# Sampling products on all 16 array tiles, column coordinates by broadcast DMA, one PSUM bank for convolution and tokens

## The chip, the cores and the metric

The kernel runs on one core of a Trainium2 chip. Times are device microseconds (us) of one execution. The core has five engines that run beside one another and meet at semaphores: TensorE (PE, with its weight loads shown as PEld), VectorE (DVE), ScalarE (ACT), GpSimd (POOL) and SyncE (SP), which here issues the DMAs. PE writes to PSUM, eight banks of 512 float32 values in each of 128 partitions; PE's array can be split into tiles of 32 rows by 32 columns. Every engine works through its own instructions in the order in which they are written.

## The reference

The input is 16 images of 64 x 64 pixels with 128 channels. Layer 0 normalises each image by groups (`_gn`), computes by a 3 x 3 convolution two offsets for every pixel and channel, and samples the normalised image bilinearly at the shifted coordinates; the result is added to the input. Layer 1 works on the 4096 tokens of an image: an attention over the 16 values of a head, with a layer norm before it, and then a mixture of experts.

```python
offsets = lax.conv_general_dilated(x, W, ...) + b            # 3x3, 128 -> 256 channels
off = offsets.transpose(0, 3, 1, 2).reshape(-1, h, w, 2)
coords = off.reshape(bc, -1, 2) + grid[None]                 # bc = image x channel
c0 = jnp.clip(coords[..., 0], 0.0, w - 1); c1 = jnp.clip(coords[..., 1], 0.0, h - 1)
# bilinear: four neighbours of (c0, c1) in the channel's own 64 x 64 plane
mapped = vals_t + (vals_b - vals_t) * f1
...
x = x + _L0_conv_ref(_gn(x), ...)
t = t + _L1_attn_ref(_ln_t(t), ...)
t = t + _L1_ffn_ref(_ln_t(t), ...)    # top 8 tokens per expert, two matmuls, scatter back
```

## The kernel before

The class `Images` takes the 16 images one after another: the first and the last written out, the fourteen between in a loop. An image has eight chunks `k` of 512 points (8 columns of the image by 64 rows); a chunk has 32 steps, called slots, and a step samples four channels (two `a`, two `h`). So an image has 256 slots, and the run 4096.

**Sampling (`sample`).** Bilinear sampling is written as sums with hat functions: the value is the sum over rows r and columns c of hat(c0 - r) hat(c1 - c) D(r, c). A hat is a ramp cut off at 0 and 1; the image is stored as differences (`xr`) so that one ramp per row and one per column is enough. A step does this:
- *Row block* (L543, tile `rps`): four bf16 matmuls spread the row coordinates of the channels, held in three bf16 parts (`parts`), over 32 rows per half image and subtract the row number.
- *Row ramp*: ACT reads the bank (L565) and ramps again in SBUF (L569); in every fourth step (`s % 4 == 2`) DVE does it in one instruction (L561). The result is `rhat`.
- *Column block* (L555, `jps`), in every second step for two steps: four bf16 matmuls do the same for the column coordinates, and ACT ramps them into `chat` (L563, L568).
- *Product block* (L501, `yps`): float32 matmuls of 32 x 32 tiles multiply the row hats with a window of 32 columns of `xr`. `half(j, 0)` does the upper half of the image's rows (row groups 0 and 1 of the array), `half(j, 1)` the lower half (row groups 2 and 3), accumulated on the upper one in the same bank. The upper half of step j+1 and the lower half of step j are issued together, on eight tiles and in two banks. An explicit dependency keeps a lower half behind the DVE product of the step before, so that only one row group writes a bank at a time.
- *Product with the column hats* (L526): DVE multiplies `yps` with min(`chat`, 1) into `prod`.
- *Sums* (L534, `acc`): every fourth step, four matmuls sum the products of four steps over the columns.

The row block of slot i is issued three slots ahead of the product of its step.

**The other work.** `conv` computes the next chunk's offsets: 18 float32 taps (L414) in two groups of nine, then DVE instructions that make and clip the coordinates, split them into bf16 parts, and DMAs that bring them to `parts`. `tokens` does layer norm, qkv, attention and gate logits of a finished chunk: transposes and matmuls on PE, large elementwise instructions on POOL (L687, L688, L692), exp on ACT (L700), sums on DVE (L701, L706). `prep` loads and normalises the next image; `tail` chooses the top 8 tokens of the image before and pools them. All these are functions put into a `Plan` under a slot number. In slot i, `plan.emit(i)` comes first, then the step's own instructions, then `plan.emit(i + 0.5)`, mostly token and convolution matmuls. So the order on each engine is this hand-made order.

**PSUM before.** Pool `bcp` has two buffers of two banks each, shared in turn by row blocks, column blocks and all token, prep and tail matmuls (`bank`); `ps_y` has two banks for the products, `ps_c` one for the convolution, `ps_a` one for the sums.

After the images, `experts` runs the two expert matmuls and `combine` scatters the results back and writes the output.

Of the kernel before, what the change touches and what calls it, by code (L numbers as in the profile page):

```python
# [18 lines left out]
P = 128  # L19
B, IMG, C = 16, 64, 128  # L20
NPIX = IMG * IMG
NCH = 8
# [15 lines left out]
TAIL_AT = [84, 88, 92, 112, 116, 120, 124, 144]  # L38
PREP_AT = [150, 154, 158, 162, 176, 180, 184, 188]
# [85 lines left out]
class Images:  # L125
# [8 lines left out]
    def __init__(self, ctx, tc, x, conv_w, conv_b, w_qkv, b_qkv, w_proj, b_proj, gate_w, gate_b,  # L134
# [7 lines left out]
        self.pc_d = dram.tile([C, 3, 2, CHW], BF16, name="pc_d")  # L142
# [5 lines left out]
        self.bcp = ctx.enter_context(tc.tile_pool(name="bcp", bufs=2, space=PSUM))  # L148
        self.ps_y = ctx.enter_context(tc.tile_pool(name="ps_y", bufs=2, space=PSUM))
        self.ps_c = ctx.enter_context(tc.tile_pool(name="ps_c", bufs=1, space=PSUM))  # L150
# [33 lines left out]
        gps = self.bank("gps")[:, 0, :E]  # L184
# [47 lines left out]

# [7 lines left out]
        self.selw = [keep([P, 8, 2 * WIN], f"selw{i}", BF16) for i in range(2)]  # L240

        self.parts = [keep([P, 4, 2, CHW], f"parts{i}", BF16) for i in range(2)]
# [6 lines left out]
        for o in range(2):  # L249
            nc.vector.memset(self.red[o], 0.0)  # L250
            rflat = self.red[o].rearrange("p t m -> p (t m)")
            for u in range(4):
                nc.vector.memset(
                    rflat[32 * u : 32 * (u + 1), 16 * (u // 2 ^ o) + u % 2 :: 34], 1.0)
# [11 lines left out]
        self.pc = keep([P, 3, 2, CHW], "pc", BF16)  # L266
# [3 lines left out]
        self.xl = keep([P, NA, C], "xl")  # L270
# [22 lines left out]
    def bank(self, name):  # L293

        return self.bcp.tile([P, 2, 512], F32, name=name, tag="bc")


    def prep(self, b, turns, slot, norm_slot):
# [4 lines left out]
        def load(t):  # L303
            nc.sync.dma_start(self.xl, xt[t])

        def turn(t):
            st["ps"] = self.bank("xps")
            for a in range(NA):
                nc.tensor.transpose(st["ps"][:, 0, P * a : P * (a + 1)], self.xl[:, a, :], self.ident)

        def stats(t):
            v = self.big[:, CHW * t : CHW * (t + 1)]
            nc.scalar.copy(v, st["ps"][:, 0, :])
# [14 lines left out]
        def group2():  # L328
            st["ps"] = self.bank("gps")[:, 0, :]
# [7 lines left out]
        def group4():  # L337
            st["ps"] = self.bank("gps")[:, 0, :]
# [33 lines left out]
        def down(r):  # L372
            st = self.xl.rearrange("p a c -> p (a c)").rearrange("p (i j) -> p i j", j=IMG)
# [32 lines left out]
    def conv(self, k, slot):  # L406
# [3 lines left out]
        def tap(s, t):  # L410
            if t == 0:
                st["ps"] = self.ps_c.tile([P, CHW], F32, name="cps", tag="c")
# [25 lines left out]
        def clip():  # L438
            nc.vector.tensor_scalar(self.cd, self.cd, 0.0, float(IMG - 1), ALU.max, ALU.min)
            nc.gpsimd.tensor_tensor(  # L440
                self.selw[k % 2].rearrange("p t (h j) -> p (t h) j", h=2),
                bcast(self.pat, 2, WIN),
                bcast(self.sgn[:, window(k) : window(k) + WIN], 1, 16), ALU.mult,
            )
# [597 lines left out]
```

## Time and profile before

| | us |
|---|---|
| median of 3 runs | 14970.91 |
| lowest and highest | 14949.8 and 14973.13 |
| profiled execution | 14941.81 |
| its span, first to last instruction | 14940.0 |
| mean granted TensorE clock | 0.836 |

Read from the trace, the images begin at about 107 us and the expert stage at about 14,198 us; the combine stage runs from 14,593 us to the end. Counting from the first DVE product of one image to that of the next, an image takes 871 to 883 us (the first 812, from 120.3 to 932.2), so a chunk takes 109 us on average and a slot 3.4. The page gives PE 78% of the span busy, DVE 61%, ACT 59%, POOL 55%. In its list of groups the number after the bar is the busy time of all instructions of a group in us, then the mean of one in ns, then the idle time of that engine just before them and what ended it. Matmuls of different tiles overlap, so the busy time of a group is not its count times its mean.

### The profile page before, as it was taken

Reading aid. Unit: us, or ns where it says so; the run is one execution under the profiler, and the core shown is the slowest. Engines: PE = TensorE matmul, PEld = TensorE weight load, DVE = VectorE, ACT = ScalarE, POOL = GpSimd, SP = SyncE. Lnnn points to the kernel's source line nnn. Section 1 sums busy time; section 2 is a strip of 40 time slices with the busy share of each in tenths; the row PEclk is TensorE's granted clock in tenths of the full one; section 3 lists DMA queues with packets and bytes.
Section 4 is the critical chain, followed back from the end, with each engine's and each line's share of the span. In section 5 each row is a group of like instructions: output and inputs, shape, how many; then the busy total and the mean of one; then the engine's idle time right before and its main releaser. Section 6 shows DMA issues by size and latency. Waiting matters only on the chain. (4 is left out here: it accounts for less than half of the span.)

```text
span 14940.0 us, 334280 instructions
## 1 busy us (share of the span) xinstructions
PE 11673.5 (78%) x144834; PEld 5414.2 (36%) x144834; DVE 9074.3 (61%) x13110; ACT 8855.4 (59%) x10818; POOL 8272.1 (55%) x5147
## 2 busy tenths in 40 slices
PE   6878777787877778777777878777777777778597
PEld 2333333333333333333333333333333333333276
DVE  4666666666666665666666566666656666665502
ACT  4666666666666666666666666666666666666400
POOL 2666565655556555565565555656566565656500
PEclk8888888888888888888888888888888888888655
DMA  1111111111111111111111111111111111111027
GB/s 43 26 38 32 35 34 34 35 30 38 32 35 34 33 35 30 33 37 35 34 33 33 34 32 36 37 30 36 30 38 32 35 37 27 37 29 35 21 92 227
DMA packets 467476, 595.25 MB, mean 40 GB/s; under 512 B 174080, under 2 KB 275200, under 8 KB 463936
## 3 DMA queue, kind: packets, MB, share of 16 engines
q1 hardware_dynamic: 429504, 539.43, 14.1%
q10 hardware_dynamic: 36480, 34.12, 0.9%
q8 instruction: 1157, 18.96, 0.5%
q14 instruction: 335, 2.74, 0.1%
HBM read 321.19 MB, written 252.18 MB: 38 GB/s over the span
## 5 line engine op out<-in xcount | busy, mean ns | idle before, releaser
L501 PE MATMUL yps<-rhat,xr 32*32 32x352 f32 (+2 forms) x98304 | 4115.0, 423 | 1299.1 <-DVE prod L526 863.1
L565 ACT ACTIVATE rhat<-rps,one 128x704 f32<-128x704 f32 x3072 | 2593.7, 844 | 3680.5 <-PE rps L543 3675.7
L526 DVE SCALAR_TENSOR_TENSOR prod<-chat,yps 128x512 f32<-128x512 f32 x4096 | 2791.8, 682 | 3035.9 <-PE yps L501 2708.7
L501 PEld LDWEIGHTS yps<-rhat,xr 32*32 32x32 f32 x98304 | 2245.6, 115 | 3471.2 <-issue 1039.1
L692 POOL TENSOR_TENSOR ev<-sc,qkv 128x1024 f32<-128x1024 f32 x1024 | 2426.1, 2369 | 1117.8 <-ACT sc L700 1012.2
L569 ACT ACTIVATE rhat<-rhat,one 128x704 f32<-128x704 f32 x3072 | 2707.1, 881 | 66.4
L414 PE MATMUL cps<-pad,wconv 128*128 128x512 f32 x4608 | 2402.0, 639 | 22.9 <-DVE far L433 16.7
L687 POOL TENSOR_TENSOR sc<-qkv 128x1024 f32<-128x1024 f32 x1024 | 1991.7, 1945 | 241.2 <-POOLq L865 106.8
L688 POOL TENSOR_TENSOR sc<-sc,top 128x1024 f32<-128x1024 f32 x1024 | 1999.5, 1953 | 82.8 <-DVE top L681 2.6
L543 PE MATMUL rps<-parts,sel 64*64 64x352 bf16 x16384 | 1538.7, 365 | 186.1 <-ACT rhat L565 136.1
L675 POOL TENSOR_TENSOR top<-qkv,kmm 128x512 f32<-128x512 f32 x128 | 136.5, 1066 | 2652.5 <-ACT qkv L671 2646.6
L706 DVE TENSOR_REDUCE att<-ev 128x64 f32<-128x1024 f32 x1024 | 1234.1, 1205 | 352.1 <-POOL ev L692 352.1
L534 PE MATMUL acc<-prod,red 128*32 128x512 f32 x8192 | 1434.0, 774 | 0.0
L563 ACT ACTIVATE chat<-jps 128x1024 f32<-128x1024 f32 x1024 | 1041.9, 1018 | 647.7 <-PE jps L555 644.0
L701 DVE TENSOR_REDUCE den<-sc 128x64 f32<-128x1024 f32 x1024 | 1241.6, 1212 | 278.4 <-ACT sc L700 275.9
L543 PEld LDWEIGHTS <-sel 64*64 64x64 bf16 x16384 | 497.2, 107 | 2278.7 <-issue 2230.7
L700 ACT ACTIVATE sc<-sc 128x1024 f32<-128x1024 f32 x1024 | 1071.6, 1047 | 211.9 <-POOL sc L688 211.9
L414 PEld LDWEIGHTS cps<-pad,wconv 128*128 128x128 f32 x4608 | 788.3, 193 | 861.0 <-issue 843.4
L568 ACT ACTIVATE chat<-jps 128x1024 f32<-128x1024 f32 x1024 | 1038.0, 1014 | 0.0
L586 POOL TENSOR_SCALAR rstd<-mv 128x4 f32<-128x4 f32 x256 | 93.7, 366 | 1661.2 <-DVE mv L583 1661.2
L555 PE MATMUL jps<-parts,selw 64*64 64x512 bf16 x8192 | 886.3, 420 | 117.9 <-ACT tr L716 88.5
L561 DVE TENSOR_SCALAR rhat<-rps 128x704 f32<-128x704 f32 x1024 | 903.7, 883 | 47.7 <-PE rps L543 47.7
(142 smaller groups left out, 10598.3 us busy)
## 6 DMA issues: line engine op xcount, KB each, us to landing
pc_d<-pc SPq DMA_DIRECT2D x128, 768.0 KB
parts<-pc_d SPq DMA_DIRECT2D x768, 128.0 KB
xl<-in_x_dram SPq DMA_DIRECT2D x128, 256.0 KB
xn_d<-xl SPq DMA_DIRECT2D x128, 256.0 KB
xr<-xn_d SPq DMA_DIRECT2D x512, 64.0 KB
xres<-in_x_dram SPq DMA_DIRECT2D x256, 128.0 KB
t_d<-t SPq DMA_DIRECT2D x256, 128.0 KB
xin_d<-xln SPq DMA_DIRECT2D x128, 256.0 KB
```

The lines of the kernel that those rows point to most:

```text
L414: nc.tensor.matmul(st["ps"], self.wconv[:, t, s, :], self.pad[:, kh + par : kh + par + 63 : 2, kw + 16 * col : kw + 16 * col + 16], start= ...
L501: mm = nc.tensor.matmul(ys[j][v : v + 32, lo:hi], self.xr[t][g : g + 32, 2 * m + a, w0 : w0 + WIN], rows[j][g : g + 32, a, lo - SEG0 * s : ...
L526: prod = nc.vector.scalar_tensor_tensor(prods[j], cols[j - j % 2][:, j % 2, :], 1.0, ys.pop(j), ALU.min, ALU.mult)
L534: nc.tensor.matmul(self.acc[32 * m : 32 * (m + 1), :], self.red[m % 2][:, t, :], prods.pop(j - 4 + m), start=(t == 0), stop=(t == 7),)
L543: nc.tensor.matmul(ps[64 * sg : 64 * (sg + 1), a, :NSEG], self.sel[64 * a : 64 * (a + 1), t, sg].rearrange("p h i -> p (h i)"), parts[64 * ...
L565: ramp = nc.scalar.activation(rows[i], ps[:, :, :NSEG], AF.Relu, bias=self.one, scale=-1.0)
L569: nc.scalar.activation(rows[i], rows[i], AF.Relu, bias=self.one, scale=-1.0)
L687: nc.gpsimd.tensor_tensor(sc, bcast(qa[:, hs], 3, HD), bcast(ka[:, hs], 2, HD), ALU.mult)
L688: nc.gpsimd.tensor_tensor(sc, sc, bcast(top[:, hs], 3, HD), ALU.subtract)
L692: nc.gpsimd.tensor_tensor(self.ev, self.sc[i % 2], bcast(va[:, hs], 2, HD), ALU.mult)
L701: add(begin[i] + 3, lambda i=i: nc.vector.tensor_reduce(den[:, 4 * i : 4 * (i + 1)], self.sc[i % 2], AX.X, ALU.add))
L706: add(begin[i] + 2, lambda j=j: nc.vector.tensor_reduce(att[:, 4 * j : 4 * (j + 1)], self.ev, AX.X, ALU.add))
```

## The change

It rewrites the sampling loop in pairs of slots and moves the PSUM banks:
- Product blocks: the upper halves of two steps and the lower halves of the two steps before them are issued together, in four banks (`ps_y` with 4 buffers), and the column tile is now `32 * (2 * a + (h ^ m % 2))`, so that two neighbouring steps use different tiles of a row group. Together they name all 16 tiles. A lower half stays behind the product of two steps before.
- The column block, `selw` and the bf16 parts of the column coordinate go. `clip` stores the float32 column coordinates in DRAM (`cc_d`); for each pair, `load_cols` reads them back with four DMAs on SP, each of which copies two rows of 512 values into 32 partitions. ACT ramps them in SBUF, with a scale and bias per partition (`csc`, `cbi`). Loads are issued three pairs ahead of their ramp.
- Row blocks have a pool of their own, `ps_r`, with one buffer of two banks.
- All token, prep, tail and convolution matmuls share the one bank of `ps_b`. For that, the qkv matmuls become four of one bank each, the second group of taps moves to slots 12 to 16, the coordinate parts follow two slots later, token work moves by one to five slots, `xl` is doubled, the tail pools two chunks at a time, and `TAIL_AT` and `PREP_AT` are new.
- The product of a step now comes six slots after its row block instead of three.

In the new file the row block is L537, DVE's row ramp L545, the DVE product L556, the product block L572, the sums L618, the taps L436.

```diff
-        self.bcp = ctx.enter_context(tc.tile_pool(name="bcp", bufs=2, space=PSUM))
-        self.ps_y = ctx.enter_context(tc.tile_pool(name="ps_y", bufs=2, space=PSUM))
-        self.ps_c = ctx.enter_context(tc.tile_pool(name="ps_c", bufs=1, space=PSUM))
+        self.ps_r = ctx.enter_context(tc.tile_pool(name="ps_r", bufs=1, space=PSUM))
+        self.ps_y = ctx.enter_context(tc.tile_pool(name="ps_y", bufs=4, space=PSUM))
+        self.ps_b = ctx.enter_context(tc.tile_pool(name="ps_b", bufs=1, space=PSUM))
...
     def bank(self, name):
-        return self.bcp.tile([P, 2, 512], F32, name=name, tag="bc")
+        return self.ps_b.tile([P, 512], F32, name=name, tag="b")
...
         def clip():
             nc.vector.tensor_scalar(self.cd, self.cd, 0.0, float(IMG - 1), ALU.max, ALU.min)
-            nc.gpsimd.tensor_tensor(
-                self.selw[k % 2].rearrange("p t (h j) -> p (t h) j", h=2),
...
-            nc.scalar.copy(self.pc[:, 0], self.cd)
+            nc.scalar.copy(self.pc[:, 0], self.cd[:, 0])
+            nc.sync.dma_start(self.cc_d[k % 2], self.cd[:, 1])
...
-        for s, at in enumerate(((0, 1, 2, 3, 4), (7, 8, 9, 11, 13))):
+        for s, at in enumerate((range(5), range(12, 17))):
...
+        def load_cols(q):
+            k, s = divmod(2 * q, STEPS)
+            t, m = divmod(s, 4)
+            cols[q] = self.hat.tile([P, 2, CHW], F32, name="chat", bufs=5)
+            for u in range(4):
+                a, h = u // 2, u % 2
+                r0 = 32 * m + 16 * a + 2 * t + h
+                step = 32 + (h ^ 1) - h
+                nc.sync.dma_start(
+                    cols[q][32 * u : 32 * (u + 1)],
+                    self.cc_d[k % 2][r0 : r0 + step + 1 : step].partition_broadcast(32),
+                )
+
+        def ramp_cols(q):
+            k = 2 * q // STEPS
+            nc.scalar.activation(
+                cols[q], cols[q], AF.Relu, bias=self.cbi[:, k : k + 1],
+                scale=self.csc[:, k : k + 1])
+
+        def ramp_rows(i):
+            k, s = divmod(i, STEPS)
+            t, m = divmod(s, 4)
...
+            ps = self.ps_r.tile([P, 2, 512], F32, name="rps", tag="r")
...
+            if m == 2:
+                nc.vector.tensor_scalar(rows[i], ps[:, :, :NSEG], 0.0, 1.0, ALU.max, ALU.min)
+            else:
+                ramp = nc.scalar.activation(
+                    rows[i], ps[:, :, :NSEG], AF.Relu, bias=self.one, scale=-1.0)
+                nc.scalar.activation(
+                    rows[i], rows[i], AF.Relu, bias=self.one, scale=-1.0)
...
+        pairs = SLOTS // 2
+        for p in range(pairs + 3):
+            for q in (0, 1) if p == 0 else (p + 1,):
+                if q < pairs:
+                    load_cols(q)
+            for e in range(2):
+                i, j = 2 * p + e, 2 * p - 6 + e
+                if 0 <= j:
+                    product(j)
+                if i < SLOTS:
+                    ramp_rows(i)
+                plan.emit(i)
+                plan.emit(i + 0.5)
+                after(i - 1)
+            if 0 <= p - 2 < pairs:
+                ramp_cols(p - 2)
+            lower = [j for j in (2 * p - 4, 2 * p - 3) if 0 <= j < SLOTS]
+            for j in (2 * p - 2, 2 * p - 1):
+                if 0 <= j < SLOTS:
+                    upper(j)
+            for lo, hi in ((SEG0, NSEG), (NSEG, CHW)):
+                for j in lower:
+                    half(j, 1, lo, hi)
...
+            if p >= 4 and p % 2 == 0:
+                j = 2 * p - 8
+                t = j % STEPS // 4
+                for m in range(4):
                     nc.tensor.matmul(
                         self.acc[32 * m : 32 * (m + 1), :], self.red[m % 2][:, t, :],
-                        prods.pop(j - 4 + m), start=(t == 0), stop=(t == 7),
+                        prods.pop(j + m), start=(t == 0), stop=(t == 7),
                     )
```

## The prediction

> **What bounds the kernel now.** I read the page's first part, then the groups by line, the waits, one undisturbed chunk in the busy times by window, the order of time, and the clock. A slot is one of the 32 steps of a chunk; a pair is two slots.
>
> The page's first part, the busy times of one chunk without tail or prep work (5305 to 5405 us), and the groups:
>
> ```profile
> PE 11673.5 (78%) x144834; PEld 5414.2 (36%) x144834; DVE 9074.3 (61%) x13110; ACT 8855.4 (59%) x10818; POOL 8272.1 (55%) x5147
> core 0: us, PE busy (x) PEld busy (x) DVE busy (x) ACT busy (x) POOL busy (x), PEclk, DMA share, GB/s
> 5305.00:5405.00 100.00, 80.66 (x1062) 34.09 (x1058) 63.57 (x93) 67.71 (x80) 62.19 (x41) 0.86 0.10 25
> L501 PE MATMUL yps<-rhat,xr 32*32 32x352 f32 (+2 forms) x98304 | 4115.0, 423 | 1299.1 <-DVE prod L526 863.1 <-ACT rhat L565 188.1 <-ACT rhat L569 154.0
> L526 DVE SCALAR_TENSOR_TENSOR prod<-chat,yps 128x512 f32<-128x512 f32 x4096 | 2791.8, 682 | 3035.9 <-PE yps L501 2708.7 <-ACT rhat L569 168.6 <-ACT pc L445 61.4
> L565 ACT ACTIVATE rhat<-rps,one 128x704 f32<-128x704 f32 x3072 | 2593.7, 844 | 3680.5 <-PE rps L543 3675.7
> L569 ACT ACTIVATE rhat<-rhat,one 128x704 f32<-128x704 f32 x3072 | 2707.1, 881 | 66.4
> L561 DVE TENSOR_SCALAR rhat<-rps 128x704 f32<-128x704 f32 x1024 | 903.7, 883 | 47.7 <-PE rps L543 47.7
> L555 PE MATMUL jps<-parts,selw 64*64 64x512 bf16 x8192 | 886.3, 420 | 117.9 <-ACT tr L716 88.5 <-ACT rhat L565 29.1
> L800 PE MATMUL wps<-ident,big 64*128 64x64 f32 x512 | 89.3, 298 | 199.7 <-ACT rhat L565 182.5 <-DVE big L780 17.2
> ```
>
> TensorE is the engine others wait for: ACT and DVE stand 3676 and 2709 us for it. But ACT and DVE themselves need 68 and 64 of the chunk's 100 us, so a shorter PE soon meets them. The last row is one of many in which PE stands until a bank of the shared ring is read.
>
> Order of time, a step at the full clock:
>
> ```profile
> 5574.10 0.85 PE L501 MATMUL yps<-rhat,xr 32*32 32x352 f32 x24
> 5574.88 0.34 PE L543 MATMUL rps<-parts,sel 64*64 64x352 bf16 x4
> 5593.67 1.44 PE L501 MATMUL yps<-rhat,xr 32*32 32x352 f32 x24
> ```
>
> From start to next start the product block takes 0.78 us, the row block 0.33 (5573.77 to 5574.10), the block of sums 1.00 (5572.77 to 5573.77); two conv taps take 1.9 in the same reading. The third row is the same product block at half clock: 1.44; the sums then take 1.94. The clock decides, and these windows, cut where the granted clock changes, show how:
>
> ```profile
> 5676.95:5680.37 3.42, 1.37 (x24) 0.99 (x27) 0.70 (x2) 3.42 (x6) 2.07 (x2) 1.00 0.00 0
> 5680.37:5683.78 3.41, 3.41 (x44) 2.34 (x34) 0.74 (x2) 2.65 (x4) 0.00 (x0) 0.50 0.01 2
> 5683.78:5687.19 3.41, 1.38 (x34) 0.66 (x29) 3.17 (x4) 1.60 (x2) 0.00 (x0) 1.00 0.10 38
> 5687.19:5690.61 3.42, 3.42 (x36) 2.33 (x40) 1.14 (x6) 0.36 (x1) 0.00 (x0) 0.50 0.31 90
> 5690.61:5694.02 3.41, 3.41 (x40) 0.99 (x36) 2.97 (x7) 1.42 (x2) 1.83 (x2) 0.50 0.09 30
> 5694.02:5697.43 3.41, 2.17 (x40) 1.16 (x32) 1.24 (x2) 3.41 (x6) 3.41 (x5) 1.00 0.00 0
> ```
>
> The second number is PE's busy time, the third from the end the clock. A window with PE busy 1.4 of 3.4 us at full clock is followed by one at half; full returns after a filled one. Counted over all windows from 912 to 13,900 us: from full clock, every one of 413 windows under 50% busy led to half, 56% of those between 50 and 60% stayed full, and all over 70%; from half clock, under 80% busy almost none came back, over 90% nine in ten did.
>
> **The change, part by part.** *Product blocks.* Two steps' upper halves and two steps' lower halves now go to 16 tiles. The block of sums already sends four different moving operands through each row group at the same pace per column, so I take one block of 0.78 plus 0.1 for twice the issues: 0.88 per pair instead of 1.56. Bounds: 0.78 and 1.56 (no gain). *Column matmuls* (L555) go: 16 blocks of about 0.3. Per chunk PE's work at full clock falls from 74 us (rows 10.6, products 25, columns 4.8, sums 8, taps 17.1, tokens about 8) to 58.
>
> *Column ramps on ACT* read SBUF instead of PSUM: 1.04 us (nearest: exp on 128x1024, 1.047) for 1.015; casts of half size give back as much. The DVE parts shrink by 1.1 us and the qkv adds grow by about 0.3. ACT stays at 67 us a chunk, DVE 63, POOL loses one 1.06 us instruction (L440). Nothing here is bound by POOL: its score stretch is 55 us over 21 slots.
>
> *The single row bank.* Before, the row block took one of two ring buffers; now rows(i+1) waits until ACT or DVE has read rows(i). In slots with m=2 the reader is DVE, after its product, which itself waits for ACT's column ramp issued at the end of the pair before. So in an odd pair ACT stands: from its first row ramp 0.85 + 0.88 + other ACT work 0.41 + column ramp 1.04 = 3.18, then product 0.68, DVE row ramp 0.88, row block 0.4, four semaphores 0.2: 5.35 us. In an even pair ACT is simply full: 3.18 + 0.85 + 0.88 + 0.41 = 5.3. A light pair therefore costs 5.35 at full clock, whatever PE does; behind PE's waiting row block stand the token matmuls and the product block, and behind those DVE's next products.
>
> *The other pairs.* Slots 0,1 / 2,3 / 14,15: PE bound, rows 0.66, four taps 3.8, products 0.88, sums 1.0 every second pair: 6.3, 5.3, 5.3. Slots 12,13: the shared bank makes the tap wait for ACT's copy of the transposes, queued behind two row ramps (0.85 + 0.88 + 0.58 + semaphores = 2.5): 8.8. Slots 16,17: the first qkv matmul waits for DVE's coordinates, behind two products, a reciprocal and a 1.2 us reduce (5.2), then 0.8 and 0.9 and part of the sums: 7.6. Slots 18,19: each qkv matmul waits for the DVE add of the one before: 7.2. With ten light pairs (one with a tap, 5.6) a clean chunk is 6.3 + 5.3 + 5.3 + 8.8 + 7.6 + 7.2 + 53.8 = 94.4 us at full clock, against 100.
>
> *The clock.* A light pair holds rows 0.66, products 0.88, half of the sums 0.5 and tokens 0.5, about 2.6 us of PE in 5.35: 48%, in the range that led to half. At half it holds about 4.4 in 5.9: 75%, which did not come back. So most light pairs run at half. The price: pairs with the sums in front of the DVE-read row block grow by 0.5 (4 pairs, 2), token matmuls stand in the open in three or four (0.9 to 1.5 each, 4), and the conv pairs at slots 0 and 12 start at half until a filled window has passed (about 5 us of half speed, 2.4 each, 5). Sum 11 (bounds 0 and 13): 105.4 us.
>
> The Trainium skill (TensorE: Matmul & The Clock Gate, Part 1 and the table of what matters for kernels) says that an idle window of about 3.4 us returns the clock to half and advises no PE gaps over about 3 us. No light pair has such a gap, so by that rule the clock would stay full and the chunk be 94.4; the windows above went to half while PE was 40% busy.
>
> *Tail, prep and image ends* make the mean chunk 109 us, 9 over the clean one. The bank waits of tail and prep matmuls (L800, L812, L309: about 500 us in the run, 3.9 a chunk) go, as each now has the bank free a slot ahead: 5.1 remain. A pipeline three pairs deep costs about 3 us more per image end, 0.4 a chunk.
>
> *DMA.* Four broadcasts a pair, 512 KB. The loop moves 34 GB/s at a share of 0.14, the last stage 244 at 0.76, so 512 KB is 1.7 to 2.2 us of all engines per pair: hidden, with three pairs between load and ramp. On SP's queue four issues (0.55 us each, as the xres load) make 2.2 us a pair; behind them stand the other loads, and ahead of them waits as long as a slot (the store of t2, the 3.9 us for pc_d). The three pairs, 16 us, cover that; without cover each late pair costs that wait. The store of the column coordinates (cc_d) waits on SP for DVE's clip, a dozen slots before its first reader, and the parts loads halve. The doubled xl, and the tail's four double turns for eight single ones, take and give single instructions: nothing.
>
> **Sum.** 105.4 + 5.1 + 0.4 = 110.9 against 109: 1.9 x 128 chunks = 240 us on the profiled 14,941.8 (span 14,940.0), so 15,180; the median of the runs stands 0.2% above the profiled run: 15,210, say 15,200.
>
> **Rivals.** *The clock holds, or half clock hides under ACT and DVE.* For it: the same loops are ACT's and DVE's, not PE's. 94.4 + 5.5 = 99.9, so 9.1 x 128 = 1165 less: about 13,800. If pairs also overlap better than I lay them out, 13,400. *The tiles don't run together* (block 1.56): 0.68 more in the six PE-bound pairs, and about 1.2 at half in three or four others, 8 us a chunk over my forecast: 16,200. Against it: the sums' four streams. *The broadcasts arrive late*, which decides from about 350 ns per 2 KB packet (16 packets per engine and 5.6 us per pair): about the same 16,200. Against it: the shares above.
>
> **Chances.** Half clock 0.47, of which 0.05 lies within 0.2% of the median (about what a measurement of this kernel can tell from no change); tiles or broadcasts 0.12; the clock or overlap helping 0.41. Slower 0.54, same 0.05, faster 0.41. The range reaches from below the first rival to the second, 13,500 to 16,200, and leaves out about a tenth on each side.
>
> **What would show it.** Right: mean granted clock in the images near 0.70 (0.85 now), product blocks near 0.9 and 1.5, ACT waiting for rows mostly after DVE row ramps, PE waits at the taps of slot 12 and at qkv. Wrong: a clock of 0.8 or more, light pairs under 5 us, product blocks of 1.5 at full clock, or ACT's column ramp waiting for its DMA.

## The result, and the profile after

The changed kernel takes 16,283.23 us (median of 4 runs, 16,279.44 to 16,289.45) where the kernel before takes 14,972.02 in the same comparison (4 runs): ratio 1.0879, 95% interval 1.086 to 1.0898. It is slower, as forecast, but by 8.8% and not by 1.5%. Its profiled execution has a span of 16,277.6 us and a mean granted clock of 0.685 (0.836 before).

The page of the changed kernel, busy times and granted clock (tenths of full speed) in 40 slices:

```profile
PE 12857.5 (79%) x136642; PEld 5127.2 (31%) x136642; DVE 8849.9 (54%) x13318; ACT 9265.4 (57%) x10754; POOL 8053.7 (49%) x5023
PEclk7676667676676766767677666667666676776655
```

PE is busier than before (12,857 us against 11,674) although 8192 column matmuls are gone: the rest runs slower. The groups by line (busy us, mean ns of one, then the idle time before them and what ended it) say of what the other engines stand:

```profile
L572 PE MATMUL yps<-rhat,xr 32*32 32x160 f32 (+2 forms) x98304 | 4406.6, 494 | 341.9 <-DVE prod L556 340.5 <-ACT rhat L547 0.3
L556 DVE SCALAR_TENSOR_TENSOR prod<-chat,yps 128x512 f32<-128x512 f32 x4096 | 2760.7, 678 | 5136.0 <-ACT chat L526 2574.7 <-issue 1095.5 <-PE yps L572 1078.9
L547 ACT ACTIVATE rhat<-rps,one 128x704 f32<-128x704 f32 x3072 | 2590.5, 843 | 4805.4 <-PE rps L537 4795.3
L526 ACT ACTIVATE chat<-chat,cbi,csc 128x1024 f32<-128x1024 f32 x2048 | 2511.9, 1228 | 3.7 <-DMA chat<-cc_d 3.7
```

L572 is the product block, L556 DVE's product, L547 ACT's row ramp, L526 the new column ramp. DVE's products now stand 5136 us and not 3036, half of it for the column ramp; ACT stands 4795 us for the row block and not 3676. The column ramp itself waits for its broadcast 3.7 us in the whole run. So the engines wait for each other in a circle, and the PE waits show where it is broken open:

```profile
PE rps L537 <- DVE rhat L545: 537.0, 533, 7.1
PE qps L695 <- DVE qkv L699: 452.7, 384, 9.6
PE qps L695 <- DVE far L455: 396.3, 126, 3.8
PE yps L572 <- DVE prod L556: 340.5, 380, 2.7
PE cps L436 <- ACT tr L691: 306.2, 126, 3.0
PE lps L687 <- POOL xln L638: 264.8, 403, 14.5
```

(Total us, times, longest.) Lines two, three and five are the one bank for conv and token work: each qkv matmul behind DVE's add of the one before (L699), the first qkv matmul behind the last instruction of DVE's coordinates (L455), the tap behind ACT's copy of the transposes (L691). The order of time on PE in slots 12 to 20 of one undisturbed chunk (rows left out between them):

```profile
5922.49 2.25 PE L572 MATMUL yps<-rhat,xr 32*32 32x352 f32 x48
5927.52 3.78 PE L436 MATMUL cps<-pad,wconv 128*128 128x512 f32 x4 [2.34 <-ACT tr L691]
5933.52 1.36 PE L572 MATMUL yps<-rhat,xr 32*32 32x352 f32 x48
5934.81 1.06 PE L618 MATMUL acc<-prod,red 128*32 128x512 f32 x8
5946.27 1.65 PE L695 MATMUL qps<-wqkv,tr 128*128 128x384 f32 x2 [3.05 <-DVE far L455]
5954.39 0.88 PE L695 MATMUL qps<-wqkv,tr 128*128 128x384 f32 x2 [2.16 <-DVE qkv L699]
5955.96 1.65 PE L695 MATMUL qps<-wqkv,tr 128*128 128x384 f32 x2 [0.29 <-DVE qkv L699]
5961.11 1.62 PE L695 MATMUL qps<-wqkv,tr 128*128 128x384 f32 x2 [0.90 <-DVE qkv L699]
```

The number in brackets is PE's idle time. A product block takes 1.36 us at full clock (1.29 to the next start) and 2.25 at half. Most of these idle times are followed by work at half clock: four taps take 3.78 us after the first wait where they take 2.0 at full clock, and the qkv matmuls 1.65 us; only those at 5954.39 run at full clock (0.88). Six windows of this stretch, cut where the clock can change (second number PE's busy us, third from the end the clock):

```profile
5910.92:5914.33 3.41, 1.91 (x48) 0.88 (x49) 3.31 (x8) 3.34 (x5) 3.27 (x2) 1.00 0.35 90
5914.33:5917.74 3.41, 3.04 (x19) 0.55 (x19) 1.98 (x7) 1.82 (x2) 3.17 (x3) 0.50 0.51 154
5927.98:5931.40 3.42, 3.42 (x8) 0.84 (x7) 0.00 (x0) 0.00 (x0) 0.27 (x1) 0.50 0.63 158
5931.40:5934.81 3.41, 3.41 (x56) 1.34 (x53) 0.00 (x0) 3.09 (x4) 0.00 (x0) 1.00 0.00 0
5941.64:5945.05 3.41, 1.58 (x10) 0.41 (x6) 3.41 (x5) 3.06 (x4) 0.00 (x0) 1.00 0.16 55
5945.05:5948.46 3.41, 2.19 (x30) 0.95 (x35) 1.17 (x3) 1.41 (x2) 0.00 (x0) 0.50 0.39 129
```

Here a window with PE 1.58 to 1.91 us busy at full clock is followed by one at half, and of the windows at half clock that are shown only one that is filled (3.42 us) brings full clock back.

And the tail of the image before, which forms pooled sums (wps, copied at L855, and pacc, L860) in slots where the tokens' last transposes (xps, L687, copied at L784) use the same bank:

```profile
5282.43 0.57 ACT L855 COPY wtT<-wps 128x512 f32<-128x512 f32 x1
5283.10 1.09 PE L687 MATMUL xps<-ident,xln 128*128 128x128 f32 x4 [2.39 <-POOL sc L732]
5286.35 0.57 ACT L784 COPY tr<-xps 128x512 f32<-128x512 f32 x1
5286.97 3.67 PE L860 MATMUL pacc<-wtT,xl 128*128 128x64 f32 x16 [2.34 <-ACT tr L784]
5290.57 2.25 PE L572 MATMUL yps<-rhat,xr 32*32 32x352 f32 x48
```

PE stands 2.39 us before the transposes and 2.34 before the pooled sums, as ACT's copy of the bank is queued behind two row ramps each time (the view names POOL for the first wait, since its instruction ended 0.04 us after the copy); then the product block starts, at half clock. This pair takes 13 us from DVE product to DVE product.

### The profile page after: what moved, and what is told of

The parts are those of the page before. It is cut to its first block, busy times and chain, and to the rows that moved or that the text cites. A ratio compares the mean times of both kernels' runs of the same rounds, so it can differ in the third digit from the quotient of the medians.

```text
span 16277.6 us, 334500 instructions
## 1 busy us (share of the span) xinstructions
PE 12857.5 (79%) x136642; PEld 5127.2 (31%) x136642; DVE 8849.9 (54%) x13318; ACT 9265.4 (57%) x10754; POOL 8053.7 (49%) x5023
## 5 line engine op out<-in xcount | busy, mean ns | idle before, releaser
L556 DVE SCALAR_TENSOR_TENSOR prod<-chat,yps 128x512 f32<-128x512 f32 x4096 | 2760.7, 678 | 5136.0 <-ACT chat L526 2574.7
L547 ACT ACTIVATE rhat<-rps,one 128x704 f32<-128x704 f32 x3072 | 2590.5, 843 | 4805.4 <-PE rps L537 4795.3
L572 PE MATMUL yps<-rhat,xr 32*32 32x160 f32 (+2 forms) x98304 | 4406.6, 494 | 341.9 <-DVE prod L556 340.5
L436 PE MATMUL cps<-pad,wconv 128*128 128x512 f32 x4608 | 2758.1, 723 | 362.9 <-ACT tr L691 306.2
L572 PEld LDWEIGHTS yps<-rhat,xr 32*32 32x32 f32 x98304 | 1785.3, 122 | 2987.9 <-issue 1970.4
L526 ACT ACTIVATE chat<-chat,cbi,csc 128x1024 f32<-128x1024 f32 x2048 | 2511.9, 1228 | 3.7 <-DMA chat<-cc_d 3.7
L537 PE MATMUL rps<-parts,sel 64*64 64x352 bf16 x16384 | 1739.5, 413 | 765.4 <-DVE rhat L545 537.0
L537 PEld LDWEIGHTS <-sel 64*64 64x64 bf16 x16384 | 550.1, 114 | 3891.8 <-issue 3820.8
L618 PE MATMUL acc<-prod,red 128*32 128x512 f32 x8192 | 1627.9, 868 | 0.0
L695 PE MATMUL qps<-wqkv,tr 128*128 128x384 f32 x1024 | 768.4, 850 | 849.7 <-DVE qkv L699 452.7
L545 DVE TENSOR_SCALAR rhat<-rps 128x704 f32<-128x704 f32 x1024 | 911.5, 890 | 777.8 <-PE rps L537 777.0
L436 PEld LDWEIGHTS cps<-pad,wconv 128*128 128x128 f32 x4608 | 894.4, 218 | 1270.3 <-issue 850.1
L638 POOL TENSOR_SCALAR xln<-t,mv,rstd 128x128 f32<-128x128 f32 x1024 | 833.4, 827 | 26.7
L462 ACT CAST pc<-cd 128x512 bf16<-128x512 f32 x128 | 79.1, 618 | 1072.3 <-DVE cd L461 1072.3
```

The lines of the kernel that those rows point to most:

```text
L436: nc.tensor.matmul(st["ps"], self.wconv[:, t, s, :], self.pad[:, kh + par : kh + par + 63 : 2, kw + 16 * col : kw + 16 * col + 16], start= ...
L526: nc.scalar.activation(cols[q], cols[q], AF.Relu, bias=self.cbi[:, k : k + 1], scale=self.csc[:, k : k + 1])
L537: nc.tensor.matmul(ps[64 * sg : 64 * (sg + 1), a, :NSEG], self.sel[64 * a : 64 * (a + 1), t, sg].rearrange("p h i -> p (h i)"), parts[64 * ...
L547: ramp = nc.scalar.activation(rows[i], ps[:, :, :NSEG], AF.Relu, bias=self.one, scale=-1.0)
L556: prod = nc.vector.scalar_tensor_tensor(prods[j], cols[j // 2][:, j % 2, :], 1.0, ys.pop(j), ALU.min, ALU.mult)
L572: mm = nc.tensor.matmul(ys[j][v : v + 32, lo:hi], self.xr[t][g : g + 32, 2 * m + a, window(k) : window(k) + WIN], rows[j][g : g + 32, a, l ...
```

## The experiments

Ratios are to the kernel before, with 95% intervals. "The changed kernel" is 1.0879 and 16,283 us.

**1. Half clock.** Zero matmuls that nothing waits for:

```diff
                 if i < SLOTS:
                     ramp_rows(i)
+                if done >= 0 and done % STEPS < 28 and not busy(i % STEPS):
+                    for _ in range(3):
+                        nc.tensor.matmul(
+                            self.acc, self.nul,
+                            self.sel.rearrange("p t s h i -> p (t s h i)")[:, :CHW],
+                            start=False, stop=False)
```

> Adds to the changed kernel, behind each row block of the slots without conv taps, three bf16 matmuls (128x128 on 128x512) of zero weights into the bank of sums: they add nothing to it, wait for nothing and take about 0.2 us each at full clock, some 12 us a chunk. Theory 'half clock': they fill the windows over 60%, the granted clock goes from 0.685 to over 0.8, and as every PE block on the path then takes its full-clock time the kernel gets faster by 3% or more (under 15,800). Theory 'loops through ACT and DVE and one row bank': the clock rises as well, but the time moves by less than 1%, since the pairs wait for ramps and not for PE.

Measured: 15,359.84 us, ratio 1.0269 (1.0252 to 1.0286), clock 0.852. PE has more to do and the kernel is 923 us faster, 5.7%: if the filler does nothing but raise the clock and take PE time, half clock is worth at least that, 7.2 us a chunk. The control, the kernel before with two such matmuls a step:

> The kernel before with two zero matmuls ahead of each row block of the slots without conv taps: the control to the filled changed kernel. Theory 'the change's loss is half clock': the kernel before, at 0.836, gains less than 2% from a clock of over 0.92 (over 14,650), where the changed kernel gained 5.7%. Rival 'both gain alike, so the clock does not tell them apart': 4% or more (under 14,400).

Measured: 14,674.47 us, ratio 0.9806 (0.9787 to 0.9824), clock 0.916. That is the first expectation, at its edge, in time (over 14,650) as in the clock (0.92): the kernel before gains 2% from the higher clock, the changed one 5.7%. Half clock is a loss that the change adds to. But at 0.852, above the 0.836 of before, the changed kernel is still 2.7% slower than before, so it is not the whole of it.

**2. Eight tiles in place of sixteen.** Each step's upper half followed by the lower halves of the step two before:

```diff
             for j in (2 * p - 2, 2 * p - 1):
                 if 0 <= j < SLOTS:
                     upper(j)
-            for lo, hi in ((SEG0, NSEG), (NSEG, CHW)):
-                for j in lower:
-                    half(j, 1, lo, hi)
+                if j - 2 in lower:
+                    for lo, hi in ((SEG0, NSEG), (NSEG, CHW)):
+                        half(j - 2, 1, lo, hi)
```

> The changed kernel with its 24 product matmuls of a pair issued as two blocks of eight tiles, one step's upper and another's lower halves each, as before the change; same four banks, same place. Theory '16 tiles bring what the blocks show': two blocks of 0.78 us start to start instead of one of 1.29, 0.27 us more a pair at full clock and 0.6 at half, where PE is on the path (about eight pairs a chunk): slower by 1.5 to 3% (16,500 to 16,800). Theory 'PE is not on the path of most pairs': within 0.7% of the changed kernel.

Measured: 16,060.4 us, ratio 1.0747 (1.0729 to 1.0765), clock 0.758. Both expectations fall: it is 1.4% *faster* than the changed kernel. Its order of time shows the blocks longer, as expected:

```profile
5910.86 1.62 PE L572 MATMUL yps<-rhat,xr 32*32 32x352 f32 x48
5917.84 0.83 PE L572 MATMUL yps<-rhat,xr 32*32 32x352 f32 x24
```

A pair's two blocks together take 1.62 us, not 1.36. Sixteen tiles bring 0.26 us a pair of PE time at full clock, and the clock goes from 0.685 to 0.758 where they are given up. That the clock is what pays is read from the two runs together with the filler's; the two issue orders differ in when the first product is ready as well.

**3. The product block nearly free.** The same words read as bf16:

```diff
+        def top(ap):
+            return ap.bitcast(BF16)[:, 1::2]
...
-                    self.xr[t][g : g + 32, 2 * m + a, window(k) : window(k) + WIN],
-                    rows[j][g : g + 32, a, lo - SEG0 * s : hi - SEG0 * s],
+                    top(self.xr[t][g : g + 32, 2 * m + a, window(k) : window(k) + WIN]),
+                    top(rows[j][g : g + 32, a, lo - SEG0 * s : hi - SEG0 * s]),
```

> The product matmuls of the changed kernel read the upper halves of the same fp32 words as bf16 (operands cut to 8 bits of mantissa): one pass instead of two, everything else is unchanged. The product block should fall from 1.36 us to 0.5 to 0.7 at full clock. Theory 'the block was sized too small and stands on the path': 0.7 to 1 us in each of the eight PE-bound pairs of a chunk and part of that in the others, 8 to 12 us a chunk: 14,700 to 15,300. Theory 'loops through ACT and DVE': light pairs stay at 5.3 us, the clock falls under 0.6 because PE has still less to do, and the time falls by under 3% (over 15,800).

Measured: 14,942.72 us, ratio 0.9996 (0.9987 to 1.0006), clock 0.656. Of 48 records 24 are left and the block takes 0.38 us at full clock and 0.52 at half. That is 0.98 to 1.73 us less a pair, 2,000 to 3,500 us over 2,048 pairs, and the kernel gets 1,340 of it, although the clock falls further. So by estimate the block stands on the path for about half of its time (1,340 of 2,000 to 3,500 us): the first theory, and its size mattered.

**4. The column ramp with constants.**

```diff
             nc.scalar.activation(
-                cols[q], cols[q], AF.Relu, bias=self.cbi[:, k : k + 1],
-                scale=self.csc[:, k : k + 1])
+                cols[q], cols[q], AF.Relu, bias=self.one, scale=-1.0)
```

> The column ramp of the changed kernel takes the constant scale -1 and the bias tile of ones instead of a scale and a bias of its own on each partition (the column weights are no longer those of the reference). Theory 'the per-partition scale costs': its mean falls from 1.23 us to the 1.05 that was forecast, 16 x 0.18 = 2.9 us a chunk, and the time by 1 to 2% (about 16,000). Rival 'it is the size, 1024 elements a partition, or the DMA writes beside it': the mean stays above 1.2 and the time within 0.5%.

```profile
L526 ACT ACTIVATE chat<-chat,one 128x1024 f32<-128x1024 f32 x2048 | 2321.9, 1135 | 3.3 <-DMA chat<-cc_d 3.3
L744 ACT ACTIVATE sc<-sc 128x1024 f32<-128x1024 f32 x1024 | 1067.7, 1043 | 108.8 <-POOL sc L732 108.8
```

Measured: 16,304.28 us, ratio 1.0902 (1.0884 to 1.0921): no gain. Three ramps of one size stand side by side: the exponential with neither scale nor bias taken from a tile 1.043 us, this ramp with a bias tile 1.135, the change's with both 1.228. Each operand read per partition costs about 0.093 us; neither expectation had that. The 190 us that ACT saves here move nothing.

**5. Without tail and preparation.** In the changed kernel (and alike in the one before):

```diff
-            plan.take(self.tail(b - 1, 66, TAIL_AT), 0, SLOTS, 0)
+            plan.add(90, lambda: nc.sync.dma_start(
+                at_image(self.wt_d, b - 1).rearrange("b e n -> (b e) n"), self.big[:E]))
...
-            plan.take(self.prep(b + 1, PREP_AT, 167, 209), 0, SLOTS, 0)
```

> The changed kernel without the tail of the image before (the top 8, the softmax over tokens and the pooled sums) and without the preparation of the next image inside the image loop; the weights of every image but the last and the pooled sums are therefore not those of the reference. Theory 'the clean chunk grew': what is left out cost what was forecast, 5.1 us a chunk, 650 us: about 15,630. Rival 'tail and preparation were under-priced, as they now share one bank with conv and tokens': 9 to 11 us a chunk, 1,150 to 1,400 us: 14,900 to 15,100.

> The kernel before with the same two parts left out. The forecast put their cost in it at 9 us a chunk, 1,150 us: 13,800 is expected. With the changed kernel's run without them it gives the change's price on the clean chunk alone: 5% by the forecast's clean chunks (105.4 against 100), 8 to 9% if the whole of the loss lies in the clean chunk.

Measured: 15,171.77 us (ratio 1.015, 1.0124 to 1.0176) and 14,189.3 us (0.9493, 0.9469 to 0.9517). The first lies between its two expectations; the second is 389 us over the 13,800 expected, so the forecast had put too much of the kernel before into these two parts. Tail and preparation cost 1,111 us in the changed kernel, 8.7 a chunk, and 783 us before, 6.1 a chunk (the clock that they let fall included: 0.723 against 0.685, 0.850 against 0.836). Without them the change still costs 982 us, 7.7 a chunk or 6.9%. Both theories have a part.

**6. The column part alone.** The kernel before with the change's broadcasts and column ramp, everything else left:

```diff
-                    pc = self.bank("jps")
-                    for e in range(2):
-                        for a in range(2):
-                            v = 64 * (a ^ e)
-                            nc.tensor.matmul(
-                                pc[v : v + 64, e, :], selw[64 * a : 64 * (a + 1), t],
...
-                    cols[i] = self.hat.tile([P, 2, CHW], F32, name="chat", bufs=3)
...
-                    nc.scalar.activation(cols[i], pc, AF.Relu)
+                    ramp_cols(i)
```

> The kernel before with the column part of the change alone: column coordinates are stored by the clip step, spread over the partitions by four DMA broadcasts a pair of steps, two pairs ahead, and turned into weights by one ACT ramp; the column matmuls go, the product blocks, the two-buffer ring and the separate conv bank stay. Theory 'the columns are not what costs': 16 blocks of 0.3 us less for PE, ACT 0.2 us a pair more: 14,300 to 15,000, the clock at 0.75 to 0.83. Rival 'the broadcasts cost (late, or SP's queue)': slower than 15,300, with DVE's products waiting for the column DMA.

Measured: 14,067.21 us, ratio 0.9406 (0.9381 to 0.9431), clock 0.82. The column part is 6% faster by itself, more than expected. The loss lies in the rest. The forecast had priced the column matmuls at 4.8 us a chunk of PE time, and about 7 are gained. The rows before and after show what else goes, the idle time before the token matmuls (qkv and the transposes of the normalised tokens):

```profile
L648 PE MATMUL qps<-wqkv,tr 128*128 128x384 f32 x1024 | 419.0, 534 | 309.7 <-DVE rhat L561 215.0 <-ACT rhat L565 94.1 <-ACT tr L643 0.7
L639 PE MATMUL lps<-ident,xln 128*128 128x128 f32 x512 | 82.1, 282 | 196.8 <-DVE rhat L561 178.0 <-POOL xln L590 17.5 <-ACT chat L563 1.3
```

```profile
L669 PE MATMUL qps<-wqkv,tr 128*128 128x384 f32 x1024 | 400.1, 514 | 0.7 <-ACT tr L664 0.7
L660 PE MATMUL lps<-ident,xln 128*128 128x128 f32 x512 | 85.5, 289 | 18.0 <-POOL xln L611 16.9 <-ACT rhat L586 1.2
```

The column block no longer takes turns in the ring of two buffers, and these matmuls hardly wait any more. How much of the gain is PE's time and how much the ring's turns, this run doesn't tell.

**7. A second bank for conv and token work.** With product work issued step by step (upper half of step i-2, lower halves of step i-4, eight tiles) three product banks are enough, and the eighth bank can go to conv and tokens:

```diff
-        self.ps_y = ctx.enter_context(tc.tile_pool(name="ps_y", bufs=4, space=PSUM))
-        self.ps_b = ctx.enter_context(tc.tile_pool(name="ps_b", bufs=1, space=PSUM))
+        self.ps_y = ctx.enter_context(tc.tile_pool(name="ps_y", bufs=3, space=PSUM))
+        self.ps_b = ctx.enter_context(tc.tile_pool(name="ps_b", bufs=2, space=PSUM))
...
+        for i in range(SLOTS + 6):
...
+            if 0 <= i - 5 < SLOTS:
+                product(i - 5)
+            if i < SLOTS:
+                ramp_rows(i)
...
+            if i % 2 == 1 and 0 <= i // 2 - 1 < pairs:
+                ramp_cols(i // 2 - 1)
+            if 0 <= i - 2 < SLOTS:
+                upper(i - 2)
+            if 0 <= i - 4 < SLOTS:
+                for lo, hi in ((SEG0, NSEG), (NSEG, CHW)):
+                    half(i - 4, 1, lo, hi)
```

> The changed kernel with its product work issued step by step (one step's upper half and the lower half of the step two before, eight tiles) so that three product banks suffice, and the eighth bank as a second one for conv and token work. Theory 'the one shared bank costs': the tap waits of slots 12 and 13, the chain of qkv and the tail's chain go, 5 to 8 us a chunk: 15,000 to 15,500. Rival 'half clock and the row bank cost': like the two blocks of eight tiles, 15,900 to 16,200.

Measured: 13,843.74 us, ratio 0.9264 (0.9239 to 0.9289), clock 0.852, faster than both kernels and than either theory said. The same loop with the pools of the change, four and one:

> The kernel with product work step by step, again with four product banks and one bank for conv and token work: it differs from the run with two such banks by that alone, and from the changed kernel by the order alone. Theory 'the shared bank costs': the tap waits at slots 12 and 13, the qkv chain and the tail's chain come back, and it is 900 us or more above the run with two banks (over 14,750). Rival 'the order by pairs costs (product blocks, sums and column ramps in one lump behind the single row bank)': within 400 us of it (under 14,250).

Measured: 15,951.47 us, ratio 1.0662 (1.064 to 1.0683), clock 0.777. Beside the changed kernel the order by steps is worth 332 us; beside the run above, the eighth bank as a fourth for products and not as a second for conv and tokens costs 2,108.

**8. The same, with the clock held up.** Two zero matmuls a step as in the first experiment, with three product banks, first with two banks for conv and tokens, then with one:

```diff
-        self.ps_b = ctx.enter_context(tc.tile_pool(name="ps_b", bufs=2, space=PSUM))
+        self.ps_b = ctx.enter_context(tc.tile_pool(name="ps_b", bufs=1, space=PSUM))
```

> The step-by-step kernel with two shared banks and two zero matmuls behind each row block of the slots without conv taps, as the run that filled the changed kernel's windows. Theory 'half clock costs here too' (granted clock 0.852 without them): clock over 0.93 and 1 to 3% faster, 13,400 to 13,700. Rival 'here PE's work at full clock is what is left, so more of it costs': 13,850 to 14,200.

> The step-by-step kernel with the zero matmuls, three product banks and one bank for conv and token work instead of two: it differs from the run of 13,764.8 us by that bank alone, with the clock held up in both. Theory 'the chain through the one bank costs by itself': 1,000 us or more over it (14,800 to 15,300) at a clock of 0.85 or more, so that about half of the 2,108 us between the runs without filler is the chain and half the clock that it lets fall. Rival 'nearly all of the 2,108 us is half clock': within 500 us of it (under 14,300).

Measured: 13,764.78 us, ratio 0.9201 (0.9183 to 0.9218), clock 0.889, the fastest version of all, between the two expectations (the clock stays under the 0.93 of the first); and 15,785.6 us, ratio 1.0555 (1.0537 to 1.0572), clock 0.829. The bank alone, nothing else changed, costs 2,021 us, 15.8 a chunk, twice what the first theory asked for, though at a clock a little under the 0.85 that it set. The run with one bank and filler is only 166 us below the one without (15,951 to 15,786; that one also had the fourth product bank), so the chain itself is what costs, with what is left of half clock (0.829 against 0.889). The filler gains only 0.6% in the version with two banks. The longest of PE's waits, the run with two banks first, then three of the longest of the run with one:

```profile
PE yps L574 <- DVE prod L558: 731.3, 921, 3.6
PE lps L695 <- POOL xln L646: 521.4, 510, 14.5
PE rps L539 <- ACT rhat L549: 311.2, 196, 3.3
```

```profile
PE qps L703 <- DVE qkv L707: 372.4, 345, 9.6
PE cps L438 <- ACT tr L699: 305.6, 126, 3.0
PE qps L703 <- DVE far L457: 215.0, 126, 2.1
```

Of the three waits of the lower list only 17 us are left with two banks: taps and qkv matmuls stand 893 us for the one bank. The rest of the 2,021 lies in the tail's chunks, as the table by chunk below shows, and, argued and not measured, in what is late behind these waits in PE's order (row blocks, and so ACT's and DVE's ramps).

## Why the forecast was right in sign and wrong in size

The forecast added 1.9 us a chunk, 240 us; 1,311 were measured, and 16,283 us is 83 above the end of its range. By experiment 5 the missing 1,071 us are 830 in tail and preparation (forecast 3.9 a chunk less, from 9 to 5.1, where 9 held the image's ends too; measured 2.6 more, from 6.1 to 8.7) and 240 in the clean chunk with the image's ends (forecast 5.8 a chunk more, measured 7.7).

Chunk by chunk, in us, from the starts of DVE's products (mean of images 1 to 14); the last two columns are the filled runs of experiment 8, which differ by one bank:

| chunk | before, bare | before | changed, bare | changed | by steps, two banks | by steps, one bank |
|---|---|---|---|---|---|---|
| 1 | 102.1 | 108.9 | 108.8 | 108.4 | 95.8 | 106.7 |
| 2 | 101.9 | 113.1 | 109.1 | 137.2 | 109.0 | 129.3 |
| 3 | 102.0 | 114.3 | 109.2 | 131.7 | 100.4 | 129.7 |
| 4 | 102.9 | 109.4 | 109.2 | 119.5 | 98.2 | 120.6 |
| 5 | 102.2 | 106.8 | 109.2 | 113.5 | 94.9 | 113.0 |
| 6 | 102.6 | 112.9 | 109.1 | 116.7 | 103.8 | 113.5 |

The tail lies in chunks 1 to 4 before and 2 to 3 after, preparation in 4 to 6.

The pairs of a clean chunk, in the same way, with each product laid to the slot that issues it: the changed kernel without tail and preparation (chunks 1 to 6), and the step-by-step runs without filler in chunk 1, in us:

| slots | forecast at full clock | changed kernel, bare | by steps, one bank | by steps, two banks |
|---|---|---|---|---|
| 2, 3 | 5.3 | 6.7 | 5.9 | 5.9 |
| 4 to 9, mean pair | 5.4 | 5.0 | 4.8 | 5.0 |
| 10, 11 | 5.35 | 8.6 | 9.8 | 10.2 |
| 12, 13 | 8.8 | 9.9 | 11.6 | 8.0 |
| 16, 17 | 7.6 | 8.5 | 7.6 | 5.3 |
| 18, 19 | 7.2 | 9.6 | 10.0 | 4.8 |
| 20, 21 | 5.35 | 6.5 | 7.2 | 4.5 |
| 28, 29 | 5.35 | 7.1 | 9.7 | 8.6 |
| chunk | 94.4, with half clock 105.4 | 109.1 | 106.6 | 95.6 |

- **The step that failed: "The bank waits of tail and prep matmuls (...) go, as each now has the bank free a slot ahead: 5.1 remain."** They have not gone; most of them were traded. PE's idle time before these matmuls, two of the rows of before (the third, L800 with 199.7, stands in the forecast) and then the three after:

```profile
L812 PE MATMUL pacc<-wtT,xl 128*128 128x64 f32 x1024 | 220.8, 386 | 164.1 <-DVE rhat L561 140.1 <-DMA xl<-xin_d 24.0
L309 PE MATMUL xps<-ident,xl 128*128 128x128 f32 x512 | 106.5, 344 | 139.7 <-ACT rhat L565 78.5 <-DVE rhat L561 33.2 <-DMA xl<-in_x_dram 28.1
```

```profile
L860 PE MATMUL pacc<-wtT,xl 128*128 128x64 f32 x1024 | 234.2, 423 | 116.9 <-ACT logits L792 36.6 <-ACT tr L784 35.1 <-PE rps L537 28.4
L329 PE MATMUL xps<-ident,xl 128*128 128x128 f32 x512 | 118.7, 375 | 135.2 <-ACT tr L784 52.5 <-ACT logits L792 37.0 <-PE rps L537 28.5
L848 PE MATMUL wps<-ident,big 64*128 64x64 f32 x512 | 76.5, 309 | 70.0 <-ACT tr L784 51.8 <-DVE big L825 17.2 <-DVE pool_sum L870 0.6
```

  504 us became 322, now mostly behind readers of the tokens (L784, L792). And taps and token matmuls (mps, pps, lps, xps of L687, gps) stand 303 us more than in the bare run, while row blocks stand 150 less. Before, conv had a bank of its own and tokens, tail and preparation took turns in the ring with rows and columns. Now they all queue in one bank, whose reader, ACT or DVE, has row ramps ahead of it. Where a step of the tail falls beside a step of the tokens, as in the pair of 13 us shown above, each matmul waits out the reader of the other. By the table by chunk it is the tail that grew: over the bare run, chunks 1 to 4 cost 37 us an image before and 60 after, chunks 5 and 6, with preparation alone, 15 and 12. And in the order by steps it is the one bank that does it: in the two filled runs chunks 2 to 4 take 20 us more than three times chunk 1 with two banks, and 60 with one. The forecast took one plan's slots at a time and never laid tail, preparation and tokens on one line.
- **The bank in the clean chunk: mechanism right, too small.** Taps behind ACT's copy and qkv behind DVE's coordinates are where the forecast put them. It priced all of it at 2.5 + 2.3 + 1.9 = 6.7 us a chunk over a pair without these waits. The filled runs put the bank at 10.9 in chunk 1 (106.7 against 95.8); the chunks with tail and preparation bring the mean to 15.8. Slots 18 to 21 show the largest miss. In the order of time above, the add of the first qkv matmul (5946.27) runs only at 5953.69, as DVE has a product and a row ramp ahead of it that wait for PE's own product and row blocks (5947.85, 5951.89). The bank's price is from the order by steps; in the order by pairs all eight banks are taken, so a second bank wasn't tried there.
- **Product block: mis-sized.** 0.88 us was taken, 1.29 to the next start was measured (1.36 in all), and 2.18 (2.25 in all) for the 1.5 at half clock. The step "0.78 plus 0.1 for twice the issues" fails: in the records of one block all 16 tiles do start within 0.1 us, but of the last eight matmuls (160 columns) one starts at 0.50 us and the other seven only from 0.80. Why these stand was not tested. By experiment 3 about half of a block's time is on the path, so the 0.41 to 0.68 us are worth some 400 to 700 us by estimate (half of 2,048 times each); light pairs that came out shorter than forecast (4.5 and 4.9 us in slots 4 to 7) took part of it back.
- **A wait that the forecast did not see:** in slots 10 and 11 the four transposes of the normalised tokens wait for POOL, one by one (lps, 265 us; 14.5 us the longest). The pair takes 8.6 us against 5.35. It is not of the shared bank: with two banks it is 10.2. Nor is the excess in slots 28 and 29 (7.1 us, 8.6 with two banks), whose cause stays open.
- **Column ramp: mis-sized, and worth nothing as far as tried.** 1.228 us for 1.04. The forecast took the duration of an exponential that has no operand from a tile. The Trainium skill (ScalarE: Activation LUTs, the section on what ACT_TABLE_LOAD costs) gives 186 ns and 0.833 ns per element, and some 93 ns for each per-partition operand: 1.225 for two of them, an estimate that the trace meets, as it does the steps in experiment 4. The kernel's time did not follow when experiment 4 took half of the excess away; ACT stands 4,795 us elsewhere.
- **The clock: its level right, its price open.** 0.69 over the images against "near 0.70". The price of 11 us a chunk (bounds 0 and 13) was not measured by itself: the filler gains 7.2 a chunk, 5.9 in the clean chunk 1 (108.4 to 102.5), with its own time still in it. And the forecast's "full returns after a filled one" holds less here than before: of the windows at half clock that PE fills (over 98% busy, from 912 to 13,000 us) 431 of 466 are followed by full clock in the kernel before and 295 of 634 in the changed one. One of the forecast's own rows (5687.19) is followed by half clock too. The Trainium skill's rule (TensorE: Matmul & The Clock Gate, Part 1), half clock after an idle window of about 3.4 us, would have kept the windows at full clock that are shown above; they were followed by half clock with PE 1.6 and 1.9 us busy. The filler's run goes against the rival of a held clock: at 0.852 the kernel is at 15,360, not 13,800.
- **The single row bank: the wait is there, the figure is not a floor.** PE waits for row banks 537 us after DVE's ramps and 185 after ACT's, and half of the 4,805 us that ACT stands before its row ramps comes right after a slot in which DVE does the ramp. But light pairs came out at 4.5 to 7.1 us for 5.35 (8.6 in slots 10 and 11), three of the ten under the 5 us that the forecast had named as a sign against it. The row bank's price by itself was not tested: every version with the new loop has it, the fastest too.
- **The DMA: right.** DVE's products wait 190 us for column broadcasts in the whole run, and experiment 6 has them in a kernel that is 6% faster. The rival of late broadcasts falls.
- **The rival "tiles don't run together"** named 16,200 us. That it lies near the measured time is luck, as its mechanism is only part of it: the block is 1.36 and not 1.56, and giving up the sixteen tiles makes the kernel faster, not slower.

So of the change's three parts the columns by DMA gain 6% in the kernel before; the sixteen tiles save 0.26 us of PE a pair and need four product banks; and the bank that conv and tokens gave up for that costs 2,021 to 2,108 us in the order by steps, more than both bring. The direction was forecast by two mechanisms that the runs show, half clock and the waits of the one bank; the size was missed because the tail, with preparation, was priced as a gain and the bank in the clean chunk too low. The Trainium skill (Perfetto Trace Analysis, Matmul Optimizations) advises that all eight PSUM banks be used. The step-by-step runs with four and one and with three and two banks (products; conv and tokens) both hold all eight; the split between them is worth 2,108 us here.

## What to carry to other kernels

Before work is moved into one shared buffer, lay every plan that uses it on one line of time, with the queue in which each reader stands: a buffer is free again when its reader's engine gets to it, not when its slot is over. A buffer taken from a chain of short dependent steps can cost more than a faster main loop brings, so try the parts of a change apart. And where the clock follows how busy PE is, a shorter block that leaves PE standing can be the slower one: price a saving at the clock that it leaves.

## What the runs showed of the hardware that was not expected

- Matmuls that compute nothing made a kernel 5.7% faster: the clock went from 0.685 to 0.852 and the time from 16,283 to 15,360 us.
- An ACT instruction of 128x1024 takes 1.043, 1.135 and 1.228 us with no, one and two operands read per partition.
- Sixteen tiles of 32x32 start within 0.1 us of each other at full clock, but of a 24-matmul fp32 block on them the last eight wait: 1.36 us, where two blocks of eight tiles take 1.62 and 0.88 had been expected.
